# Layer 0 of a two-layer AdaLN block: 32 queries of four heads share a score matmul, and the stage begins in a written order on one load queue

## The chip, the cores and the metric

The kernel runs on one NeuronCore of a Trainium2 chip. The metric is the device time of one execution in microseconds (us). Before the change three runs took 1959.87, 1960.4 and 1962.59 us: a median of 1960.4 us. One core has five engines with queues of their own: TensorE (PE; its weight loads are listed as PEld), VectorE (DVE), ScalarE (ACT), GpSimd (POOL) and SyncE (SP), which here only issues DMAs. SBUF is the working memory of 128 partitions; PSUM has eight banks of 512 f32 columns per partition, into which PE writes.

## The reference, cut to what matters

The program is a two-layer block with adaptive layer norm on 1024 tokens of 512 features, all in f32. The change lies in the first half of layer 0:

```python
mod = (_silu(L0_c) @ L0_wmod).reshape(L0_c.shape[0], 6, 1, -1)
sa, ca, ga, sb, cb, gb = (mod[:, 0], mod[:, 1], mod[:, 2], mod[:, 3], mod[:, 4], mod[:, 5])
...
h = _layernorm(x, axis=-1) * (1 + ca) + sa
x = x + ga * _L0_attn_ref(h, ...)
```

The attention dequantizes its weights (`(qw - 8) * scales`, one scale for 128 rows), makes 32 query heads and 8 key and value heads of 128 features, turns q and k by rotary tables, and computes for each query head

```python
scores = jnp.einsum('bhqd,bhkd->bhqk', q, k) / math.sqrt(HD)
scores = jnp.where(causal[None, None], scores, jnp.finfo(scores.dtype).min)
attn = jax.nn.softmax(scores.astype(jnp.float32), axis=-1).astype(q.dtype)
ctx = jnp.einsum('bhqk,bhkd->bhqd', attn, v)
```

Four query heads (a *group*) share one key and one value head. The context goes through a dequantized output projection. A gated feed-forward network, a second attention with small heads and a mixture of low-rank experts follow; the change does not touch them.

## The kernel before

The code is written for a library that records the operations in program order, works out all dependencies and semaphores, and then lets a planner place the operations on the engines: it takes what is ready by its own model of costs, the earlier in the program the sooner. So each engine's queue is in order on the chip, but that order is the planner's, not simply that of the code. Outside a block of written order (there is none before the change) an operation may be placed ahead of earlier ones. A buffer pool with n buffers makes the n+1st tile wait until the first is released.

**The start** (L92 to L480). `load_x(0)` brings tokens 0 to 511 over SP; x is held as eight tiles of 128 tokens. The vector c arrives twice over ACT's queue, as a column (`cc`, L384) and spread over all partitions (`crow`, L386); then come four tiles `wa` of the modulation weight for the shift (L390) and four tiles `wm` for the scale (`mod_loads`, L117). Each of these tiles is 256 KB. `cc` and `row` are multiplied by their sigmoids. `ln_stats` computes the statistics of four token tiles and the normalized `xn`; `ln_transposes` turns `xn` into four PSUM banks, one of 128 features by 512 tokens each, 16 transposes (L416); the shift comes from 16 matmuls with one moving column each (L446), the scale from four multiply-and-sum operations on DVE (`mod_sums`, L124); `ln_evict` writes hT (L424 on ACT, L429 on DVE). Then follow the first K projection (`project_rope`, L204 on PE; L210, L212, L213 on DVE; the addition L214 on POOL), the V projection (L248), and the same for the second half of the tokens. The loads of weights and tables go over SP (L184, L185, L192, L194, L236, L238).

**The loop over groups.** For each of 8 groups and each of 8 query tiles of 128 (`order`: 7, 0, 6, 1, 5, 2, 4, 3 and, in the last group, 3, 7, 2, 6, 1, 5, 0, 4) a *step* does the following. For each of the four heads `head_probs` streams the (qi+1)*128 keys past that head's 128 queries (L293, pieces of at most 512 columns into a tile of two PSUM banks, three such tiles), adds the causal mask to the last 128 columns (L298), takes the maximum (L300), the exponential with its sum (L303), the reciprocal (L308) and scales (L309). `transpose_probs` transposes blocks of 32x32 in place on DVE (four operations, L315), and 16 DMAs (L317, on SP) carry them into `pT`, with the keys on the partitions. Two steps later `context` (L326) multiplies by v, ACT copies the result (L332), and `project_o` (L337, L342, L343) adds to x. `drain` puts these after the second and the fourth head's scores. The tiles `pr` and `pT` have one buffer for the big steps (qi 4 to 7) and one for the small ones.

**Work beside the steps.** `side_work` prepares the next group: at step 0 the K weight is loaded, at step 1 K is projected, at step 2 V (every second group), at step 3 the first two query heads are projected, at step 5 the third, at step 6 the output weight is loaded and at step 7 the fourth query head is projected. Before the first group all four query heads are projected one after the other (L204), followed by the output weight and the gate. `qT` holds one tile of 1024 columns per head, eight buffers.

In the trace each f32 matmul of the code is two records, the transposes are one.

Of the kernel before, what the change touches and what calls it, by code (L numbers as in the profile page):

```python
# [9 lines left out]
F32 = mybir.dt.float32  # L10
# [3 lines left out]
ALU = mybir.AluOpType  # L14
AX = mybir.AxisListType
# [27 lines left out]
def block_kernel(ctx: ExitStack, tc: tile.TileContext, a: dict, out: bass.AP):  # L43
# [48 lines left out]
    load_x(0)  # L92
# [4 lines left out]
    make_causal_mask(nc, cmask, mask_val=NEG)  # L97
    eps_t = const.tile([P, 1], F32, tag="eps", name="eps_t")
# [66 lines left out]
    with ExitStack() as st:  # L165
# [33 lines left out]
        def project_rope(dst, wf, halves=(0, 1)):  # L199

            for half in halves:
# [11 lines left out]
                nc.vector.tensor_mul(t2[64:128, :], ps[0:64, :], sinT[0:64, sl])  # L213
                nc.gpsimd.tensor_tensor(dst[:, sl], t1, t2, ALU.add)  # L214
# [39 lines left out]
        def project_q(h):  # L254
            qT[h] = qp.tile([P, S], F32, tag="qT", name="qT")
            project_rope(qT[h], wf.pop(("q", h)))
# [12 lines left out]
        class Step:  # L269


            def __init__(self, g, qi):
# [9 lines left out]
                self.pr, self.pT = (  # L282
                    t[:, :used].rearrange("p (b r k i) -> p b r k i", b=NB, r=REP, i=B)
                    for t in (pr, pT)
                )

        def head_probs(u, r):

            nk = u.n * P
            ps = sp.tile([P, S], F32, tag="sc", name="sc")  # L290
            for n0 in range(0, nk, 512):
                w = min(512, nk - n0)
                nc.tensor.matmul(  # L293
                    ps[:, n0 : n0 + w], lhsT=qT[u.g * REP + r][:, bass.ts(u.qi, P)],
                    rhs=kT[u.g][:, n0 : n0 + w], start=True, stop=True,
                )
            dg = ps[:, u.qi * P : nk]
            nc.vector.tensor_tensor(dg, dg, cmask, ALU.add)  # L298
            nb = small.tile([P, 1], F32, tag="nb", name="nb")
            nc.vector.tensor_reduce(nb, ps[:, :nk], AX.X, ALU.max, negate=True)  # L300
            rs = small.tile([P, 1], F32, tag="rs", name="rs")
            pr = u.pr[:, :, r, :, :]
            nc.scalar.activation(  # L303
                pr.rearrange("p b k i -> p k b i"),
                ps[:, :nk].rearrange("p (k b i) -> p k b i", b=NB, i=B),
# [5 lines left out]
        def transpose_probs(u):  # L311

            for b in range(NB):
                t = u.pr[:, b, :, :, :].rearrange("p r k i -> p (r k i)")
                nc.vector.transpose(t, t)  # L315
                for q in range(NB):
                    nc.sync.dma_start(  # L317
                        u.pT[b * B : (b + 1) * B, q, :, :, :].rearrange("p r k i -> p (r k i)"),
                        t[q * B : (q + 1) * B, :],
                    )  # L320

        def context(u):

            ps = psum_mm()
            for kj in range(u.n):
                nc.tensor.matmul(  # L326
                    ps, lhsT=vv[u.g][:, kj, :],
                    rhs=u.pT[:, :, :, kj, :].rearrange("p a r i -> p r a i"),
# [891 lines left out]
```

## Time and profile before

| what | value |
|---|---|
| median of three runs | 1960.4 us |
| the profiled execution | 1962.43 us, of which 1960.7 us from its first to its last instruction (the span) |
| mean granted clock of PE | 0.975 |
| first record on PE | 17.30 us after the start of the span |
| first K projection | 30.44 us |
| first scores | 87.3 us |
| last context of layer 0 | 1143.3 us |
| feed-forward network of layer 0, gate and up | from 1164.2 us |

The page gives busy time per engine, the groups of instructions by code line with their mean length in ns, and the idle time of the engine before them with what ended it. `sc<-kT,qT 128x512` means that the tile sc is written from kT and qT with 512 columns on 128 partitions. The timeline lists start, length, engine, line, operation and count; in brackets is the idle time before, and what ended it. The length of a matmul record includes its way through the array, so two records that follow each other overlap; the distance of their starts is their cost in a row (0.43 us for 512 columns, by 24 records of L204 in 10.46 us).

### The profile page before, as it was taken

Reading aid. Unit: us, or ns where it says so; the run is one execution under the profiler, and the core shown is the slowest. Engines: PE = TensorE matmul, PEld = TensorE weight load, DVE = VectorE, ACT = ScalarE, POOL = GpSimd, SP = SyncE. Lnnn points to the kernel's source line nnn. Section 1 sums busy time; section 2 is a strip of 40 time slices with the busy share of each in tenths; the row PEclk is TensorE's granted clock in tenths of the full one; section 3 lists DMA queues with packets and bytes.
Section 4 is the critical chain, followed back from the end, with each engine's and each line's share of the span. In section 5 each row is a group of like instructions: output and inputs, shape, how many; then the busy total and the mean of one; then the engine's idle time right before and its main releaser. Section 6 shows DMA issues by size and latency. Waiting matters only on the chain.

```text
span 1960.7 us, 21062 instructions
## 1 busy us (share of the span) xinstructions
PE 1842.4 (94%) x6582; PEld 874.5 (45%) x6582; DVE 1175.9 (60%) x2632; ACT 664.5 (34%) x1392; POOL 225.1 (11%) x192
## 2 busy tenths in 40 slices
PE   5989999999999999999998879999988999999987
PEld 4434454444544444544443434444554344334434
DVE  4766757677666767576776542323456577667432
ACT  1134424434334343244335410000113323355530
POOL 0211111111111212111110110002000000000010
PEclk9999999999999999999999989999989889999999
DMA  5344435345533445343444360001001000000001
GB/s 188 118 111 136 122 99 135 91 126 147 132 91 86 112 130 127 99 135 91 127 131 101 87 244 0 0 1 49 0 1 63 8 10 7 4 7 7 5 12 38
DMA packets 93856, 155.77 MB, mean 79 GB/s; under 512 B 25232, under 2 KB 38160, under 8 KB 93744
## 3 DMA queue, kind: packets, MB, share of 16 engines
q1 hardware_dynamic: 91424, 149.17, 28.4%
q10 hardware_dynamic: 1440, 2.36, 0.4%
q0 software_dynamic: 880, 2.88, 0.4%
q8 instruction: 53, 0.87, 0.2%
q14 instruction: 59, 0.48, 0.1%
HBM read 74.38 MB, written 2.36 MB: 39 GB/s over the span
## 4 chain that ended last, share of the span: by engine, by line
PE 71%; DVE 15%; DMA 4%; ACT 4%; issue 3%; SPq 2%; POOL 1%; DVEq 0%; ACTq 0%; POOLq 0%
PE mm L204 10%; PE mm L337 9%; PE mm L326 8%; PE sc L637 8%; PE sc L293 8%; PE sc L821 5%; PE sc L870 4%; PE sc L656 4%; PE ctx L894 3%; PE sc L731 2%; DVE q L832 2%; PE mm L248 2%; DVE nb L300 2%; DVE pr L315 2%; SPq L317 2%
## 5 line engine op out<-in xcount | busy, mean ns | idle before, releaser
L303 ACT ACTIVATE pr<-sc,nb 128x1024 f32<-128x1024 f32 (+7 forms) x256 | 187.6, 735 | 419.5 <-DVE nb L300 319.0
L204 PE MATMUL mm<-hT,wf 128*128 128x512 f32 x640 | 283.4, 594 | 3.1 <-DVE t L213 2.8
L326 PE MATMUL mm<-pT,v 128*128 128x512 f32 x576 | 264.2, 604 | 21.2 <-DMA pT<-pr 21.2
L293 PE MATMUL sc<-kT,qT 128*128 128x512 f32 (+3 forms) x768 | 273.7, 487 | 7.5 <-ACT pr L303 7.5
L337 PE MATMUL mm<-wo,ctxT 128*128 128x512 f32 x512 | 237.7, 603 | 11.4 <-ACT ctxT L332 11.2
L293 PEld LDWEIGHTS sc<-kT,qT 128*128 128x128 f32 x768 | 139.3, 190 | 157.9 <-issue 125.2
L309 ACT ACTIVATE pr<-pr,rs 128x1024 f32<-128x1024 f32 (+7 forms) x256 | 187.9, 768 | 51.7 <-DVE rs L308 51.4
L315 DVE STREAM_TRANSPOSE pr<-pr 128x1024 f32<-128x1024 f32 (+7 forms) x256 | 177.7, 747 | 20.4 <-ACT pr L309 19.3
L300 DVE TENSOR_REDUCE nb<-sc 128x1 f32<-128x1024 f32 (+7 forms) x256 | 187.6, 750 | 3.5
L204 PEld LDWEIGHTS mm<-hT,wf 128*128 128x128 f32 x640 | 121.1, 191 | 153.6 <-issue 142.1
L883 ACT ACTIVATE pspace<-sc 128x512 f32<-128x512 f32 (+3 forms) x303 | 126.9, 503 | 163.6 <-PE sc L877 117.9
L326 PEld LDWEIGHTS mm<-pT,v 128*128 128x128 f32 x576 | 110.0, 194 | 146.9 <-issue 130.5
L832 DVE CUSTOM_DVE_ANT_0 q<-sc,cwide 128x512 f32<-128x512 f32 (+3 forms) x256 | 125.5, 490 | 66.7 <-PE sc L821 42.2
L821 PE MATMUL sc<-kv,q 32*128 32x512 f32 (+3 forms) x768 | 154.5, 536 | 11.2 <-DVE mx L832 9.7
L343 POOL TENSOR_TENSOR x<-x,ot 128x512 f32<-128x512 f32 x64 | 83.1, 1299 | 667.8 <-DVE ot L342 562.9
L637 PE MATMUL sc<-hT,gu 128*128 128x512 f32 x352 | 153.1, 594 | 0.0
L337 PEld LDWEIGHTS mm<-wo,ctxT 128*128 128x128 f32 x512 | 94.6, 191 | 128.4 <-issue 92.6
L870 PE MATMUL sc<-q,kv 32*128 32x512 f32 (+3 forms) x768 | 112.8, 574 | 4.2 <-DVE mx L837 2.0
L214 POOL TENSOR_TENSOR qT<-t,t 128x512 f32<-128x512 f32 x64 | 87.2, 1363 | 175.8 <-DVE t L213 175.8
L308 DVE RECIPROCAL rs<-rs 128x1 f32<-128x1 f32 x256 | 37.6, 156 | 112.7 <-ACT pr L303 111.9
L637 PEld LDWEIGHTS sc<-hT,gu 128*128 128x128 f32 x352 | 66.2, 190 | 85.2 <-issue 79.6
L821 PEld LDWEIGHTS sc<-kv,q 32*128 32x128 f32 x768 | 73.9, 190 | 57.9 <-DVE mx L832 25.9
(174 smaller groups left out, 1763.5 us busy)
## 6 DMA issues: line engine op xcount, KB each, us to landing
pT<-pr SPq DMA_DIRECT2D x128, 128.0 KB, 2.4
pT<-pr SPq DMA_DIRECT2D x128, 112.0 KB, 2.2
pT<-pr SPq DMA_DIRECT2D x128, 96.0 KB, 2.1
wm<-in_wmodT_dram SPq DMA_DIRECT2D x40, 256.0 KB, 2.8
pT<-pr SPq DMA_DIRECT2D x128, 80.0 KB, 2.1
wi<-in_qw_q_dram SPq DMA_DIRECT2D x32, 256.0 KB, 4.1
ws<-in_s_q_dram SPq DMA_DIRECT2D x32, 256.0 KB, 3.8
oi<-in_qw_o_dram SPq DMA_DIRECT2D x32, 256.0 KB, 3.5
```

The source lines that it names most:

```text
L204: nc.tensor.matmul(ps, lhsT=wf[:, c, :], rhs=hT[half][:, c, :], start=(c == 0), stop=(c == NC - 1),)
L293: nc.tensor.matmul(ps[:, n0 : n0 + w], lhsT=qT[u.g * REP + r][:, bass.ts(u.qi, P)], rhs=kT[u.g][:, n0 : n0 + w], start=True, stop=True,)
L300: nc.vector.tensor_reduce(nb, ps[:, :nk], AX.X, ALU.max, negate=True)
L303: nc.scalar.activation(pr.rearrange("p b k i -> p k b i"), ps[:, :nk].rearrange("p (k b i) -> p k b i", b=NB, i=B), AF.Exp, bias=nb, accum ...
L309: nc.scalar.activation(pr, pr, AF.Copy, scale=rs)
L315: nc.vector.transpose(t, t)
L326: nc.tensor.matmul(ps, lhsT=vv[u.g][:, kj, :], rhs=u.pT[:, :, :, kj, :].rearrange("p a r i -> p r a i"), start=(kj == 0), stop=(kj == u.n ...
L337: nc.tensor.matmul(ps, lhsT=u.ctxT[:, r, :], rhs=wo[u.g][:, r, :], start=(r == 0), stop=(r == REP - 1),)
L637: nc.tensor.matmul(ps, lhsT=gu[:, j, m, c, :], rhs=hTc[b][:, c, :], start=(c == 0), stop=(c == NC - 1),)
L821: nc.tensor.matmul(banks[r][:, at : at + w], lhsT=u.q[kp, bass.ts(i, P)], rhs=kT1[kp, u.g, n0 : n0 + w], start=True, stop=True,)
L832: nc.vector.tensor_tensor_reduce(sm[:, :w], ps, cwide[:, 512 - w :], 1.0, -3e38, ALU.add, ALU.max, accum_out=u.mx[:, i, r, 0:1],)
L870: nc.tensor.matmul(banks[r][:, :w], lhsT=kT1[kp, u.g, bass.ts(kb, P)], rhs=u.q[kp, q0:QW], start=True, stop=not diag,)
```

## The change

It has three parts.

1. *The start.* All that is between `ordered = ...manual_schedule()` and `first.close()` keeps, on each engine, the order in which it is written. The loads all go over SP, in the order cc, crow, first half of x, scale weights, shift weights, K weight, tables, V weights, second half of x, second half of the tables, first q weight. The shift is computed as a row: four matmuls with `cc` as the stationary operand and 512 moving columns, a copy to SBUF (`srow`), four transposes of one row each, and a copy to a column. The 16 transposes of `xn` go token tile by token tile. `load_k(0)` is written ahead of the eviction. `ln_stats` is divided in two, and the statistics of the second half lie between two pairs of V projections.

2. *The scores.* `qT` is one tile for a group, with columns ordered by block of 32 queries, then head, then query; POOL writes each head's part in pieces of 32. `probs(u, s)` takes 32 queries of all four heads as the 128 stationary columns, for s = 0 to 3. It streams only the keys up to the last of these queries, (qi*128 + 32s + 32), fills the rest of the last 128 columns with -1e30 on DVE for s < 3, adds a 128x32 mask (`cmask4`, made by four small copies at the start), and takes the maximum over the streamed columns alone. The exponential still covers (qi+1)*128 columns. `pr` and `pT` are laid out anew: the four DVE transposes and the 16 DMAs of a step keep their sizes, and the moving operand of the context matmul is read in pieces of 128 in place of 32.

3. *The fourth query head* is projected at step 5 with the third, and no longer at step 7.

```diff
-    load_x(0)
...
+    cmask4 = const.tile([P, 32], F32, tag="cmask4", name="cmask4")
+    for r in range(REP):
+        rows = slice(32 * r, 32 * r + 32)
+        nc.vector.tensor_copy(cmask4[rows, :], cmask[rows, rows])
...
         def project_q(h):
-            qT[h] = qp.tile([P, S], F32, tag="qT", name="qT")
-            project_rope(qT[h], wf.pop(("q", h)))
+            g, r = divmod(h, REP)
+            if r == 0:
+                qT[g] = qp.tile([P, S // B, REP, B], F32, tag="qT", name="qT")
+            project_rope(qT[g][:, :, r, :], wf.pop(("q", h)))
...
+        def probs(u, s):
+            nk = u.n * P
+            d0 = u.qi * P + B * s
+            ps = sp.tile([P, S], F32, tag="sc", name="sc")
+            q = qT[u.g][:, NB * u.qi + s, :, :].rearrange("p r i -> p (r i)")
+            for n0 in range(0, d0 + B, 512):
+                w = min(512, d0 + B - n0)
+                nc.tensor.matmul(
+                    ps[:, n0 : n0 + w], lhsT=q, rhs=kT[u.g][:, n0 : n0 + w], start=True, stop=True
                 )
...
+            if s + 1 < NB:
+                nc.vector.memset(ps[:, d0 + B : nk], NEG)
+            dg = ps[:, d0 : d0 + B]
+            nc.vector.tensor_tensor(dg, dg, cmask4, ALU.add)
             nb = small.tile([P, 1], F32, tag="nb", name="nb")
-            nc.vector.tensor_reduce(nb, ps[:, :nk], AX.X, ALU.max, negate=True)
+            nc.vector.tensor_reduce(nb, ps[:, : d0 + B], AX.X, ALU.max, negate=True)
...
             elif i == 5:
                 project_q(h0 + 2)
+                project_q(h0 + 3)
             elif i == 6:
                 load_o_weight(g + 1)
-            else:
-                project_q(h0 + 3)
...
+        ordered = first.enter_context(tc.manual_schedule())
         cc = fp.tile([P, NC], F32, tag="cc", name="cc")
-        nc.scalar.dma_start(cc, a["c0"])
+        nc.sync.dma_start(cc, a["c0"])
         row = const.tile([P, D], F32, tag="crow", name="crow")
-        nc.scalar.dma_start(row, a["crow0"].partition_broadcast(P))
+        nc.sync.dma_start(row, a["crow0"].partition_broadcast(P))
+        load_x(0)
+        scales = mod_loads(0, 1, nc.sync)
         wa = []
         for k in range(NC):
             wa.append(fp.tile([P, D], F32, tag=f"wa{k}", name=f"wa{k}"))
-            nc.scalar.dma_start(wa[k], a["wmodS"][bass.ts(k, P), :])
-        scales = mod_loads(0, 1, nc.scalar)
+            nc.sync.dma_start(wa[k], a["wmodS"][bass.ts(k, P), :])
...
-        xn = ln_stats(0)
+        xn = ln_norm(0, *stats)
+        mod_sums(0, 1, scales)
+        ps = psum_mm()
+        for k in range(NC):
+            nc.tensor.matmul(
+                ps[0:1, :], lhsT=cc[:, k : k + 1], rhs=wa[k], start=(k == 0), stop=(k == NC - 1)
+            )
+        srow = fp.tile([1, D], F32, tag="srow", name="srow")
+        nc.scalar.copy(srow, ps[0:1, :])
         banks = ln_transposes(xn)
         ps = psum_mm()
...
+        for c in range(NC):
+            nc.tensor.transpose(ps[:, c : c + 1], srow[:, bass.ts(c, P)], ident[0:1, 0:1])
         mod[0, 0] = const.tile([P, NC], F32, tag="mcol00", name="mcol00")
...
+        nc.vector.tensor_copy(mod[0, 0], ps[:, :NC])
+        load_k(0)
         ln_evict(0, banks)
-        load_k(0)
         load_tables(0)
+        vf, v = load_v(0)
         load_x(1)
-        vf, v = load_v(0)
         load_tables(1)
         kT[0] = kvp.tile([P, S], F32, tag="kT", name="kT")
         project_rope(kT[0], wf["k", 0], (0,))
-        project_v(vf, v, range(4))
-        xn = ln_stats(1)
+        project_v(vf, v, range(2))
+        stats = ln_stats(1)
+        xn = ln_norm(1, *stats)
+        project_v(vf, v, range(2, 4))
```

## The prediction, on record before the change was run

> **What bounds the kernel now.** I read four views in this order: the busy shares and groups of the page, the windows of the layer-0 loop, the waits of TensorE (PE), and the first 45 us as a timeline. The page first:
>
> ```profile
> PE 1842.4 (94%) x6582; PEld 874.5 (45%) x6582; DVE 1175.9 (60%) x2632; ACT 664.5 (34%) x1392; POOL 225.1 (11%) x192
> ...
> L293 PE MATMUL sc<-kT,qT 128*128 128x512 f32 (+3 forms) x768 | 273.7, 487 | 7.5 <-ACT pr L303 7.5
> ```
>
> PE is busy 94% of the span, and the score matmuls (L293) hardly ever wait (7.5 us in 768). A share over the whole span can hide a stage with another limit, so the windows of single groups of the attention come next (columns: length, then busy time of PE, PEld, DVE, ACT, POOL, granted clock, DMA share, GB/s):
>
> ```profile
> 150.00:280.00 130.00, 128.34 (x354) 65.24 (x353) 85.92 (x180) 53.84 (x109) 20.66 (x16) 1.00 0.47 125
> ...
> 410.00:540.00 130.00, 127.90 (x348) 64.18 (x347) 90.37 (x182) 50.95 (x101) 22.34 (x17) 1.00 0.51 135
> ...
> 1040.00:1150.00 110.00, 90.28 (x227) 41.60 (x226) 59.95 (x134) 47.90 (x93) 11.22 (x10) 0.95 0.42 102
> ```
>
> In groups 0 to 6 PE works 128 of 130 us, VectorE (DVE) about 90, ScalarE (ACT) about 53: there PE time taken away is time gained. The last group (from about 1040) has 20 us of PE idle time; the waits say for what:
>
> ```profile
> PE mm L326 <- DMA pT<-pr: 21.2, 5, 7.1
> PE mm L446 <- DMA x<-in_x_dram: 17.3, 1, 17.3
> ```
>
> The context matmuls wait for the transposed probabilities, a latency. The second line is the start of the kernel, the other place where PE does nothing. Its timeline (start, length, engine, line):
>
> ```profile
> 1.64 5.30 ACTq L390 DMA_DIRECT2D wa<-in_wmodS_dram  x4
> ...
> 12.14 1.28 ACT L435 ACT_TABLE_LOAD   x1 [12.14 <-DMA wm<-in_wmodT_dram]
> ...
> 17.30 6.99 PE L446 MATMUL mm<-cc,wa 128*128 128x1 f32 x32 [17.30 <-DMA x<-in_x_dram]
> ...
> 26.44 3.65 PE L416 MATMUL tr<-ident,xn 128*128 128x128 f32 x16 [2.15 <-DVE xn L405]
> ...
> 42.20 1.91 PE L416 MATMUL tr<-ident,xn 128*128 128x128 f32 x16
> ```
>
> ACT issues loads until 12.1 and computes nothing before. DVE, in order, sits behind the second half of x (until 16.49), so cc is multiplied at 17.11 and PE begins at 17.30. The first K projection starts at 30.44.
>
> **Scores (the main term).** Each code matmul is two records in this trace. Shapes of L293, kept apart (busy, mean ns):
>
> ```profile
> L293 PE MATMUL sc<-kT,qT 128*128 128x512 f32 x384 | 187.3, 594 | 4.3 <-ACT pr L303 4.3
> ...
> L293 PE MATMUL sc<-kT,qT 128*128 128x384 f32 x128 | 50.5, 488 | 2.6 <-ACT pr L303 2.6
> ...
> L293 PE MATMUL sc<-kT,qT 128*128 128x128 f32 x128 | 22.5, 274 | 0.0
> ```
>
> 128 columns are worth 594-488 = 106 ns, and (488-274)/2 = 107: 0.835 ns a column. A step now streams (qi+1)*128 columns four times; after the change 128qi+32, +64, +96, +128. That is 96+64+32 = 192 columns less, 160 ns a record, 0.32 us for the two records. But a narrow matmul need not be cheap: L446 took 6.99/32 = 218 ns for one column, L416 3.65/16 = 228 ns for 128 columns, both near each other in the first 30 us, where the same 16 transposes took twice what they took at 42.20 (1.91). One column costs what 128 cost, so the weight load sets a floor at 128 columns. In qi = 0 and qi = 4 all four last pieces are 32 to 128 wide: no gain. Six of eight steps gain, 48 in eight groups: 15.4 us. The six of the last group (1.9) fall where PE waits anyway; I count none of them: **-13.5**. Both ends: without the floor another 16*0.32 = 5.1 (then up to -20.5); with all gain lost to waits, 0.
>
> The Trainium skill ("TensorE: Matmul & The Clock Gate", Back-to-back issue gap) lists about 60 cycles (25 ns) for 1 to 64 columns, so by it the narrow pieces would gain too, about 5 us more. The rows above speak for the floor.
>
> **Beside them on DVE and ACT.** The mask add shrinks from 128x128 (290 ns) to 128x32. A 128x4 add takes 145 to 162, so about 185: 256*105 = 27 us less. The maximum reads 48 columns less on average; from 411 ns (256 wide) to 1222 (1024) it is 1.06 ns a column: 13 us less. New are 192 memsets of 32 to 96 columns in PSUM, an operation that the trace has only in SBUF (85 ns at 32 columns, 59 at one): 112 ns by that slope, at most 290 by the mask row, 21 to 56 us. DVE ends between 19 us less and 16 more, of 90 in 130 us: hidden under PE either way. Exponentials, scaling (row forms with pieces of 32 are already in the 128-wide steps: 396 ns against 360), the transposes and the 16 copies per step keep size and count: 0. q is now written in pieces of 32 on POOL; the trace has no such store. Between today's 1.27 us and twice that, it stays under the 3.43 us that PE needs for a half (8 records of 0.43): 0.
>
> **The start.** The first 8 us move 195 to 408 GB/s, from then on 387 whoever issues, also after 13.4, when SP alone issues. So one queue loses nothing, and the order decides. Adding up 2 us windows: 0.4 MB by 4 us, 0.85 by 6, 1.66 by 8, 2.46 by 10, 3.2 by 12. In the new order x half 0 is complete (1.3 MB) at 7.1, scales (2.4) at 9.7, wa0 (2.6) at 10.4, wa3 (3.4) at 12.4, K weights (3.9) at 13.8. ACT is free to take its tables at once, cc is ready near 4, xn at 10.7 (4 statistics to 8.1, root, 1.9 us of xn). PE then runs 8 records of 512 columns. At the slow start they cost 0.86 each: 10.5 to 17.3 (15.5 if the clock rises on the way); copy of srow 0.6; the 16 transposes beside it 3.4 (or 1.9), 4 small ones 0.8 (0.4); then on DVE the column copy 0.2, which the K dequantization (0.7 to 0.9) is queued behind, and an eviction of 0.8. K starts at 20 to 23.3 instead of 30.44. The chain of half 1 is longer than before (rope 2.1, v eviction, statistics 3.7, xn 1.9, all in order on DVE, PE idle about 2 us before the transposes): K half 1 at 35.7 to 38.7 instead of 43.95, 5 to 8 earlier. I take **-6**, with ends -9 and 0 (the q phase has DVE busy 9.7 to 9.9 of 10 us from 70 on, which may swallow part).
>
> The rule of the same page (Part 1) is that the clock doubles after about 3.4 us of sustained activity; then wa would end at 15.5. Row L446 ran 7 us at 218 ns without rising, which speaks against counting on it; the difference is 1.8 us.
>
> **First scores wait for four heads.** Today heads 0 to 2 are scored at 87.42, while q3's last half leaves POOL at 90.84. DVE gets to the first mask at 89.64 only. New: PE at 90.9, first mask at 92.7, and project_k(1), ready by 85.6, fills PE meanwhile. Context 0 (115.19, after 5.49 idle) comes 1 to 3 us later: **+2** (ends 0 and 5).
>
> **q3 one step sooner.** It issues no load; its 16 records (6.86 us) and six rope multiplies move from step 7 to 5. So steps 7 and the next 0 lose cover. In one group, step 6's last score is at 331.53, its copies land at 347.3 (15.8 us later), and its context begins at 356.47. Of the 24.9 us between, 6.86 go away, 1.6 were idle, 0.3 is saved in scores: 16.1 of work against 15.8. SP needs 22.93 us for the 32 copies of steps 6 and 7 (0.62 to 0.7 each). The margin is gone, hardly more: 0.4 us at 7 boundaries, **+3** (ends 0 and 36).
>
> **Sum**, against the profiled execution (1962.43, span 1960.7 and 1.7 around it): -13.5-6+2+3 = -14.5, 1947.9. The median of the runs is 2.0 below that execution, so the median after should be **1946** (own range 1938 to 1953).
>
> **Rivals.** (1) *Start lost, scores kept*: DVE as the bound at 70 to 90 eats the earlier start. For: 9.85 of 10 us busy. Against: only two slices. -13.5+5 = -8.5: 1952. (2) *Scores not converted*: memset, mask and maximum hold the three score banks longer, and PE waits for the exponential (today 7.5 us) where it had columns. Then -6+5 and a little: 1958. (3) *All better*: no floor, start -9, boundaries free: -13.5-5-9+2: 1935. (4) *Slower*: at each of the 7 boundaries PE runs dry until pT lands. It decides from 2.5 us a boundary (17.5/7). With 3.5 us idle and the half clock that followed such a gap at 601 us (3.4 us at 0.5, 1.7 lost), 7*5.2 = 36: 1978. Against: the chain is 15.8 us under work of 16.1, and the rope multiplies leave it. (5) The written order might not hold on the chip as written, or the planner, which places all that follows, shuffles the loop to a wash: 1960.
>
> **Chances.** Forecast 0.52, (1) 0.17, (2) 0.08, (3) 0.10, (4) 0.08, (5) 0.05. A measurement of this kernel tells 0.2% (4 us) from no change. (2) is half faster, half same: faster 0.83, same 0.08, slower 0.09. The range leaves out (4), (5) and the ends of the others: 1934 to 1958.
>
> **What would show it.** Right: L293 columns 13 to 16 us less busy, idle time before L326 and L293 nearly as now between 150 and 1040; K projection at 20 to 24; first mask near 93. Wrong: L293 busy falls and idle time before L326 at the boundaries grows by more than 2 us each (4); the narrow matmuls well under 110 ns apart (3); DVE at the boundaries without gaps (2).

## The result, and the profile after

The changed kernel takes **1969.1 us** in the median of 19 runs (1964.89 to 1976.76); the kernel before, in the same session, 1961.17 us (19 runs, 1959.3 to 1965.49). The ratio is 1.0041, with a 95% interval of 1.0032 to 1.005. The change makes the kernel 0.4% slower. The forecast was 1946 us, the range ended at 1958: time and sign were wrong. The profiled execution of the changed kernel has a span of 1966.4 us (1960.7 before) and a mean granted clock of 0.969 (0.975).

The page of the changed kernel, in the groups that answer to those shown of before (busy us, mean ns, then the idle time before them and its releaser):

```profile
PE 1836.5 (93%) x6562; PEld 864.1 (44%) x6562; DVE 1165.5 (59%) x2828; ACT 667.0 (34%) x1393; POOL 225.3 (11%) x192
...
L349 PE MATMUL mm<-wo,ctxT 128*128 128x512 f32 x512 | 244.3, 617 | 29.1 <-ACT ctxT L344 28.5
L304 PE MATMUL sc<-kT,qT 128*128 128x512 f32 (+15 forms) x768 | 262.2, 471 | 9.7 <-ACT pr L315 9.0
```

PE is busy 6 us less, the scores 11.5 us less (273.7 to 262.2): most of the forecast saving is there, though the sign that the prediction named was 13 to 16 us. The span is longer all the same, so idle time was added. The waits of PE in the changed kernel (sum, times, longest) say where:

```profile
PE mm L349 <- ACT ctxT L344: 28.5, 26, 2.7
PE mm L338 <- DMA pT<-pr: 20.1, 9, 6.9
PE mm L462 <- DMA wa<-in_wmodS_dram: 11.9, 1, 11.9
```

The wait for pT is what it was (21.2 before), the wait at the start is 5.4 us shorter (the forecast had PE begin at 10.5 us, it began at 11.91). New is the first line: the output projection waits for the copy of the context, 28.5 us. Its counterpart before:

```profile
PE mm L337 <- ACT ctxT L332: 11.2, 17, 2.1
```

The windows of the loop (length, then PE, PEld, DVE, ACT, POOL busy, clock, DMA share, GB/s):

```profile
150.00:280.00 130.00, 125.88 (x344) 63.29 (x343) 83.84 (x202) 54.07 (x109) 18.98 (x15) 0.99 0.46 123
410.00:540.00 130.00, 125.99 (x333) 61.33 (x332) 89.49 (x207) 52.47 (x104) 22.06 (x17) 0.99 0.47 127
1040.00:1150.00 110.00, 90.77 (x230) 41.67 (x228) 63.78 (x176) 51.92 (x102) 10.15 (x8) 0.97 0.40 98
```

PE fell from 128 to 126 of 130 us, and the clock from 1.00 to 0.99. DVE is no busier in the first two, and PE's time in the last group hardly changed. The loss is in groups 0 to 6, and PE does not spend it on work.

**One boundary, side by side.** A *boundary* is the place where step 7 of a group ends and step 0 of the next begins. Here is that of the third group on PE. Before (start, length, engine, line, operation, count; in brackets idle time before and releaser):

```profile
346.17 7.03 PE L204 MATMUL mm<-hT,wf 128*128 128x512 f32 x16
353.04 3.60 PE L293 MATMUL sc<-kT,qT 128*128 128x512 f32 x8
356.47 4.46 PE L326 MATMUL mm<-pT,v 128*128 128x512 f32 x10
360.76 3.60 PE L293 MATMUL sc<-kT,qT 128*128 128x512 f32 x8
364.20 3.60 PE L337 MATMUL mm<-wo,ctxT 128*128 128x512 f32 x8
```

The same window after:

```profile
351.01 4.99 PE L304 MATMUL sc<-kT,qT 128*128 128x512 f32 x12
355.84 4.46 PE L338 MATMUL mm<-pT,v 128*128 128x512 f32 x10
360.13 1.88 PE L304 MATMUL sc<-kT,qT 128*128 128x512 f32 x4
364.69 5.40 PE L349 MATMUL mm<-wo,ctxT 128*128 128x512 f32 x8 [2.69 <-ACT ctxT L344]
```

Before, the fourth query head (16 records) precedes the new step, and the new step's 16 score records stand as 8 ahead of the context and 8 between context and output projection. After, nothing precedes it, and the planner sets 12 ahead and leaves 4 between. The 4 last 1.7 us; then PE is idle for 2.69. ACT in that window, after:

```profile
359.51 2.19 ACT L321 ACTIVATE pr<-pr,rs 128x1024 f32<-128x1024 f32 x2 [0.33 <-DVE rs L320]
361.61 1.09 ACT L315 ACTIVATE pr<-sc,nb 128x1024 f32<-128x1024 f32 x1
...
363.02 1.15 ACT L321 ACTIVATE pr<-pr,rs 128x1024 f32<-128x1024 f32 x1 [0.23 <-DVE rs L320]
364.08 0.57 ACT L344 COPY ctxT<-mm 128x512 f32<-128x512 f32 x1
```

The context is complete at 360.3, but ACT is in order: from 359.5 on it has three scalings and an exponential of the new step ahead of the copy, which begins at 364.08. Before, it began earlier, while PE still had scores to 364.4:

```profile
363.17 0.57 ACT L332 COPY ctxT<-mm 128x512 f32<-128x512 f32 x1
```

After the change, the eight output projections take 5.40 us in place of 3.60, and the clock tells why, in the window of these records:

```profile
364.70:368.30 3.60, 3.60 (x5) 1.58 (x6) 0.16 (x1) 2.20 (x3) 0.00 (x0) 0.54 0.01 3
```

The same gap (2.15, then five of 2.68 or 2.69 us) stands at 220, 365, 494, 636, 764 and 909 us, one for each boundary up to that of group 6; four of the six were followed by 3.4 us at half clock.

**The account of seven groups**, from the first context of group 0 to that of group 7: 936.9 us before, 944.8 after, +7.9. Distances of score records at full clock -13.0 (221.1 to 208.1). Idle time of PE +13.1 (22.4 to 35.5; the wait for ctxT alone 9.4 to 25.6). Lost to half clock +4.2 (8.7 us at half clock, later 17.1). The remaining 3.6 is spread over the other records. The last group takes 91.8 us (91.2), the part behind layer 0 812.5 (812.4), and the first context comes 2.9 earlier.

### The profile page after: what moved, and what is told of

The parts are those of the page before. It is cut to its first block, busy times and chain, and to the rows that moved or that the text cites. A ratio compares the mean times of both kernels' runs of the same rounds, so it can differ in the third digit from the quotient of the medians.

```text
span 1966.4 us, 21175 instructions
## 1 busy us (share of the span) xinstructions
PE 1836.5 (93%) x6562; PEld 864.1 (44%) x6562; DVE 1165.5 (59%) x2828; ACT 667.0 (34%) x1393; POOL 225.3 (11%) x192
## 4 chain that ended last, share of the span: by engine, by line
PE 69%; DVE 16%; ACT 5%; DMA 4%; SPq 3%; issue 2%; POOL 1%; DVEq 0%; POOLq 0%; ACTq 0%
PE mm L208 11%; PE mm L349 9%; PE sc L657 8%; PE mm L338 7%; PE sc L304 6%; PE sc L841 5%; PE sc L890 4%; PE sc L676 4%; PE ctx L914 3%; DVE pr L327 3%; ACT pr L321 2%; DVE nb L312 2%; DVE q L852 2%; SPq L329 2%; PE sc L751 2%
## 5 line engine op out<-in xcount | busy, mean ns | idle before, releaser
L349 PE MATMUL mm<-wo,ctxT 128*128 128x512 f32 x512 | 244.3, 617 | 29.1 <-ACT ctxT L344 28.5
L304 PE MATMUL sc<-kT,qT 128*128 128x512 f32 (+15 forms) x768 | 262.2, 471 | 9.7 <-ACT pr L315 9.0
L312 DVE TENSOR_REDUCE nb<-sc 128x1 f32<-128x384 f32 (+31 forms) x256 | 175.6, 703 | 3.5
L320 DVE RECIPROCAL rs<-rs 128x1 f32<-128x1 f32 x256 | 38.7, 158 | 106.4 <-ACT pr L315 103.8
```

The source lines that it names most:

```text
L304: nc.tensor.matmul(ps[:, n0 : n0 + w], lhsT=q, rhs=kT[u.g][:, n0 : n0 + w], start=True, stop=True)
L312: nc.vector.tensor_reduce(nb, ps[:, : d0 + B], AX.X, ALU.max, negate=True)
L349: nc.tensor.matmul(ps, lhsT=u.ctxT[:, r, :], rhs=wo[u.g][:, r, :], start=(r == 0), stop=(r == REP - 1),)
```

## Experiments

The theory from this profile: **cover**. Without the fourth query head between step 7 and step 0, PE arrives too early and some wait surfaces (work that keeps PE busy while another engine finishes is its cover). Its rivals: the **loop is paced by ACT and DVE**, so saved columns are worth nothing; the **first scores wait for all four heads**; and, as a theory of its own, the **order** of records on PE at the boundary. The letters of the expectations are each text's own. "Seven" is the time from the first context of group 0 to that of group 7, "last" from there to the start of the last context, in the one profiled run of each kernel, in us.

```
variant                                      median us   ratio [95%]              seven  last
before                                       1961.17                              936.9  91.2
after                                        1969.1    1.0041 [1.0032, 1.005]     944.8  91.8
e4  start alone                              1960.98   0.999  [0.9976, 1.0003]    934.2  96.2
e6  scores alone                             1989.78   1.013  [1.0112, 1.0148]    956.3  98.1
e3  fourth head at step 5 alone              1970.26   1.0041 [1.0028, 1.0053]    942.1  94.2
e5  after, old start                         1978.38   1.0077 [1.0062, 1.0092]    941.8  97.8
e1  after, fourth head at step 7             1987.34   1.0125 [1.011, 1.014]      957.3  95.3
e2  after, fourth head at step 6             1958.79   0.9976 [0.9966, 0.9987]    929.1  93.6
e12 after, all columns streamed              1971.71   1.0041 [1.0027, 1.0055]    940.5  94.0
e7  after, context copied by DVE             2019.39   1.0287 [1.0262, 1.0312]    995.8  93.8
e9  after, K projected at step 0             1977.15   1.0083 [1.0057, 1.011]     951.6  91.3
e10 after, hold                              1971.93   1.0041 [1.0026, 1.0056]    933.5 101.7
e11 e2 and hold                              1962.01   0.9994 [0.9984, 1.0005]    928.8 102.9
e14 after, hold in groups 0 to 6             1955.86   0.9958 [0.9942, 0.9974]    933.1  92.7
e13 after, fourth head in halves, 6 and 7    1957.0    0.9977 [0.9967, 0.9988]    929.7  93.8
e15 e13 and hold in groups 0 to 6            1947.44   0.9918 [0.9902, 0.9934]    923.2  96.2
e16 before, start, fourth head at step 6     1963.41   0.9998 [0.9989, 1.0007]    937.5  92.8
e17 before, hold in groups 0 to 6            1975.29   1.0062 [1.0047, 1.0077]    946.4  94.0
e18 before, start, halves, hold              1972.98   1.0052 [1.0036, 1.0067]    948.1  95.3
```

Two things for reading the table. Many expectations missed: the times of e1, e3, e5, e6, e7, e9, e14, e17 and e18 lie outside every range that they gave, those of e2 and e15 by less than 1 us. And the part behind layer 0, the same code in all variants, took from 808.9 us (e15) to 816.8 (e10) in the profiled runs, 812.4 before and 812.5 after, with 74 to 98 us at half clock. So differences of a few us between medians need not come from the edit; where it matters, the column "seven" decides.

### The three parts alone

**e4**, the kernel before with part 1 of the diff alone.

> The kernel before with the first part alone: written order and one load queue. In the changed kernel the query projections began 6.6 us earlier (48.4 for 55.0). Theory A and B alike: the loop is as before, so 1961 - 6.6 = 1954 to 1955; if DVE at 60 to 90 us eats it, 1957 to 1961.

1960.98 us; the interval of the ratio includes 1. The first context comes 6.8 us earlier (108.4), the seven groups gain 2.7, but the last group takes 5.0 more and the part behind layer 0 3.9 more (816.3 against 812.4, with 98 against 81 us at half clock). What the start gains arrives at the loop, and most of it is not in the end; why the later stages took longer in that run is not settled.

**e6**, part 2 alone (old start, fourth head at step 7).

> The kernel before with the second part alone: 32 queries of four heads in a score matmul, the fourth query head at step 7, old start. The streamed columns fall by 19 to 20 us by the distances of the records in the changed kernel. Theory A: nearly all of that is gained, less 2 to 5 us because the first scores wait for four heads: 1944 to 1949. Theory B: the wait for ctxT appears here, 1962 to 1975. A third theory, C: with four heads in a piece the projection at step 7 itself stands in the way of the next group's first scores (rope and POOL before them, about 4 us a group): 1961 - 20 + 28 = 1965 to 1972, with the idle time before L293's successor and not before the output projection.

1989.78, the slowest of the parts. The waits of PE:

```profile
PE sc L305 <- POOL qT L222: 20.9, 8, 3.2
PE mm L350 <- ACT ctxT L345: 18.8, 27, 2.1
```

Six of the eight waits are of 3.24 us, at the boundaries up to that of group 6: the first stacked scores need the fourth head, whose last half POOL stores only then (from 359.19 to 360.95 us, for scores that begin at 361.01). The rival of the four heads holds wherever the fourth head stands at step 7.

**e3**, part 3 alone.

```diff
                 project_q(h0 + 2)
+                project_q(h0 + 3)
             elif i == 6:
                 load_o_weight(g + 1)
-            else:
-                project_q(h0 + 3)
```

> The kernel before with the third part alone: the fourth query head is projected at step 5, scores per head as before, old start. Theory A: the boundary wait appears here too, so PE's wait for ctxT rises from 11 to about 30 us and the time by 15 to 30 us: 1976 to 1991. Theory B: no new wait, 1957 to 1965.

1970.26, 0.41% slower, with the scores and the start of before.

```profile
PE mm L337 <- ACT ctxT L332: 20.2, 26, 1.7
```

The wait for ctxT goes from 11.2 to 20.2 us, that for pT does not move (20.4). At the boundaries the planner writes the same order as in the changed kernel, 12 score records ahead of the context and 4 behind it, with gaps of 1.63 to 1.75 us. The fourth head's step alone costs 8 us, of which, by the profiled runs, 5.2 lie in the seven groups and 3.0 in the last. Moving it is what makes part 2 usable, and it has a price of its own.

**e5** and **e1**, the changed kernel without part 1, and without part 3 (the fourth head back at step 7).

> The changed kernel with the old start (parts two and three alone). The kernel with the start alone was 2 us faster than the one before, inside its interval, though its first context came 6.8 us earlier; the changed kernel's came 2.9 earlier. If the start is worth what the trace shows at the first context, this kernel is 3 to 6 us slower than the changed one: 1972 to 1975; if half-clock stretches later give it back, 1967 to 1971.

> The changed kernel with its third part undone: the fourth query head is projected at step 7 again. Theory A (the moved projection): the 6.9 us of PE work that stood at step 7 were the time in which ACT and DVE caught up before the next group's first step; without them the copy of the context to ctxT sits behind the exponentials on ACT and PE waits (2.69+0.68+0.30+0.56 = 4.2 us a group, and often a half clock of 3.4 us after the longest). Then this kernel loses that wait at seven boundaries: 1969 - 7*(3 to 4) = 1941 to 1948. Theory B (the stacked scores themselves cause the wait: three banks are held by pieces that all end at nearly the same time, and memset, mask and maximum come between): this kernel keeps the wait of ctxT near 28 us and lies within 4 us of 1969.

1978.38: in the changed kernel the new start is worth 0.36%, 7 us. 1987.34: the same eight waits for POOL's qT (20.9 us) as in e6.

**e2**, the fourth head at step 6, between the two.

```diff
             elif i == 5:
                 project_q(h0 + 2)
-                project_q(h0 + 3)
             elif i == 6:
+                project_q(h0 + 3)
                 load_o_weight(g + 1)
```

> The changed kernel with the fourth query head projected at step 6, between the places tried so far (5 in the changed kernel: PE waits 2.7 us for ctxT at a group boundary; 7 in the run before: PE waits 3.2 us for q from POOL). Theory A+C (the projection is the only spare PE work near the boundary: too late it stands before the first scores, too early it leaves the copy of the context behind the exponentials): at step 6 its rope and POOL work end 9 us before the next scores, and step 7 begins 6.9 us later, so step 0 meets an ACT that has caught up. No wait for POOL, and the wait for ctxT falls from 28 to 15 us or less: 1950 to 1958. Theory B (the stacked scores stall at the boundary wherever the projection is): 1964 to 1975.

1958.79, 0.24% faster than before. Up to the boundary of group 6 none has a gap of over 0.7 us; the seven groups take 929.1, 15.7 less than in the changed kernel, for the same instructions. The boundary of the third group on PE:

```profile
350.27 2.47 PE L304 MATMUL sc<-kT,qT 128*128 128x416 f32 x6
352.57 4.46 PE L338 MATMUL mm<-pT,v 128*128 128x512 f32 x10
356.87 3.54 PE L304 MATMUL sc<-kT,qT 128*128 128x512 f32 x8
360.25 3.60 PE L349 MATMUL mm<-wo,ctxT 128*128 128x512 f32 x8
```

Moving this one line turns the sign. But two things change with it: the projection stands nearer to the boundary, and the planner sets 8 score records between context and output projection again. Of the variants without the hold introduced below, those with the fourth head at step 5 (after, e3, e5, e7, e9, e12) all have 12 and 4, the others all 8 in between.

### What paces the boundary

**e12**, all (qi+1)*128 columns streamed and the maximum taken over them, with four 128x128 masks and no memset: the stacked scores without their saving.

```diff
-            for n0 in range(0, d0 + B, 512):
-                w = min(512, d0 + B - n0)
+            for n0 in range(0, nk, 512):
+                w = min(512, nk - n0)
...
-            if s + 1 < NB:
-                nc.vector.memset(ps[:, d0 + B : nk], NEG)
-            dg = ps[:, d0 : d0 + B]
-            nc.vector.tensor_tensor(dg, dg, cmask4, ALU.add)
+            dg = ps[:, u.qi * P : nk]
+            nc.vector.tensor_tensor(dg, dg, cmask4[s], ALU.add)
```

> The changed kernel without the saving of columns: pieces of 32 queries of four heads, but all (qi+1)*128 keys streamed, one mask of 128x128 for each of the four pieces, no memset, the maximum over all columns. PE has 17 us more to stream. If PE sets the pace in the loop, 1969 + 17 = 1983 to 1987. If the loop waits on the chain over ACT and DVE at the boundaries, PE's longer scores fill the gaps: 1966 to 1975, with less idle time before the output projection.

The same ratio, 1.0041. In the changed kernel the whole saving is worth nothing: with 13.6 us more of score records in the seven groups (208.1 to 221.7), these take 4.3 us less (940.5), the boundary gaps shrink from 2.69 us to between 1.63 and 1.75, and no half clock follows them. PE is not what sets the pace at that place.

**e7**, the copy of the context on DVE, to take it out of ACT's queue.

```diff
-            nc.scalar.copy(u.ctxT.rearrange("p r q -> p (r q)"), ps)
+            nc.vector.tensor_copy(u.ctxT.rearrange("p r q -> p (r q)"), ps)
```

> The changed kernel with the copy of the context to ctxT on DVE in place of ACT (DVE about 0.4 us for 256 columns from PSUM, so 0.7 for 512). Theory A: what PE waits for at the boundary is a place in ACT's queue, behind the exponentials of the next group's first step. On DVE the copy stands behind shorter work (maxima of 1.2 us), so the wait for ctxT falls, by 7*2 us and the half clocks that follow: 1950 to 1960. If not the place in the queue counts but the whole load of ACT and DVE at the boundary, the wait moves to DVE and the time stays at 1965 to 1973.

2019.39, 2.9% slower.

```profile
PE sc L304 <- ACT pr L315: 48.5, 23, 4.4
PE mm L349 <- DVE ctxT L344: 29.5, 17, 3.4
```

On DVE, in order too, the copy stands behind reciprocals that wait for ACT's exponentials (3.28 us idle ahead of one at 375.9 us) or behind 4.6 us of transposes, and the masks and maxima behind it come later, so the scores wait for their banks. It is again a short copy in a queue of longer work.

**e9**, the K weight loaded a group ahead and K projected at step 0 in place of 1.

> The changed kernel with other PE work at the boundary: the K weight is loaded one group ahead at step 6, and K is projected at step 0 in place of step 1 (same 16 records, 6.9 us, not needed before the next group). In this kernel's order they stand right behind the first output projection of the group. Theory A: spare work at the boundary is what is missing. The first wait for ctxT (2.69) stands before these records on PE and may stay, the following ones (0.68, 0.3, 0.56) go: 1960 to 1967. If PE's order takes them before the output projection, 1948 to 1955.

1977.15, worse. The gaps for ctxT remain (23.6 us, longest 2.7): the 16 records of K stand behind the copy that is waited for. Work helps only if it stands ahead of it.

### The order on PE

**e10** and **e11**: the third score matmul of each step (s = 2) may be issued only behind the last context matmul before it. So at most 8 of the 16 large score records go ahead of a context, and 8 stay behind it. e10 is the changed kernel with this hold, e11 is e2 with it.

```diff
+                with tc.issue_after(held[0].ins) if s == 2 and held[0] is not None else ExitStack():
                     nc.tensor.matmul(
                         ps[:, n0 : n0 + w], lhsT=q, rhs=kT[u.g][:, n0 : n0 + w],
                         start=True, stop=True,
                     )
...
-                nc.tensor.matmul(
+                held[0] = nc.tensor.matmul(
                     ps, lhsT=vv[u.g][:, kj, :],
```

> The changed kernel with one order fixed by hand: the third score piece of a step is queued on PE behind the last context matmul of that step. In the changed kernel the planner puts three of the four pieces of a group's first step ahead of the context, so only four records (1.7 us) are left between the context and the output projection, which waits 2.7 us for the copy to ctxT; in the kernel before it was eight (3.4 us). Theory A1 (the wait is this order): the wait at the boundary falls under 1.3 us at once and the time to 1955 to 1961. Theory A2 (as my prediction priced its rival: without the projection at step 7 the transposed probabilities are not there in time): PE now waits in front of the context for pT by about as much, and the time stays at 1965 to 1973.

> The kernel with the projection at step 6 (1958.8, wait for ctxT 18 us) with the same order fixed by hand. There the planner had put the third piece behind the context already at the boundary, so A1 expects little: 1953 to 1960. If holding pieces back costs elsewhere (ACT gets its exponentials later in every step), 1961 to 1968.

1971.93 and 1962.01: nothing gained. The first reading, that the order does not matter, was wrong, and only the division by groups shows it. (In e11 the seven groups stay where e2 has them, 928.8 and 929.1: there 8 records already stood between.) In e10 the seven groups gain 11.3 us (944.8 to 933.5) and the last group loses 9.9 (91.8 to 101.7): there PE waits for pT anyway, and the hold keeps the scores from filling that wait. The waits of e10:

```profile
PE mm L342 <- DMA pT<-pr: 34.5, 12, 8.2
...
PE mm L353 <- ACT ctxT L348: 11.1, 14, 1.7
```

**e14** takes the hold out of the last group alone (`if s == 2 and u.g + 1 < NKV and ...`).

> The changed kernel; in groups 0 to 6 the third score matmul of a step (s of 2) is issued only behind the last context matmul before it, as in the run with the hold in all groups; group 7 keeps the planner's order. In that run the seven groups took 933.5 us from first context to first context (944.8 in the changed kernel), and the last group 101.7 (91.8). Theory D (the loss in groups 0 to 6 is an order in which too few scores stand between context and output projection; the hold's own cost fell in the last group alone): the seven groups near 934, the last near 92, so 1959 to 1963 us. Theory A (cover is lost, and the hold only exchanges one wait for another): seven groups at 940 to 945, 1966 to 1972 us.

1955.86, 0.42% faster than before and 0.8% faster than the changed kernel. The seven groups as in e10, 11.7 us under the changed kernel, the last at 92.7: the order is a cause by itself. Its boundary on PE:

```profile
354.54 3.33 PE L305 MATMUL sc<-kT,qT 128*128 128x512 f32 x8
359.19 4.53 PE L342 MATMUL mm<-pT,v 128*128 128x512 f32 x10 [1.31 <-DMA pT<-pr]
363.55 3.54 PE L305 MATMUL sc<-kT,qT 128*128 128x512 f32 x8
366.93 3.60 PE L353 MATMUL mm<-wo,ctxT 128*128 128x512 f32 x8
```

8 and 8 again: no gap at ctxT, and in its place one of 0.8 to 1.8 us at pT, the wait that the prediction had named. Behind the order the missing cover appears. By two single runs it is the smaller part: e2, with 8 between as well and no wait for pT at these boundaries, is another 4.0 us lower in the seven groups (933.1, 929.1).

**e13** gives it back without the wait of e1: the half of the tokens that the next group's first step reads is projected at step 6, the other at step 7.

```diff
             elif i == 6:
+                project_q(h0 + 3, (0,) if g + 2 == NKV else (1,))
                 load_o_weight(g + 1)
+            elif i == 7:
+                project_q(h0 + 3, (1,) if g + 2 == NKV else (0,))
```

> The changed kernel, but the fourth query head is projected in two halves: the half of the tokens that the next group's first step reads at step 6, the other half at step 7 (8 records each, so cover stands ahead of the boundary again, and the first scores of the next group wait only for the half of step 6). Theory A (the boundary has lost its cover, and some wait surfaces there, of the copy of ctxT or of pT): the gap of 2.7 us before L349 at the boundary shrinks to under 1 us, no wait for POOL's qT of over 1 us appears, 1950 to 1957 us, at least 0.4% under the kernel before and not above the variant with the whole head at step 6 (1958.8). Theory B (what is lost is lost in the loop as a whole, on ACT and DVE, wherever the fourth head stands): 1958 to 1968 us, with the waits moved elsewhere. Theory C (the first scores wait for the whole of POOL's qT whatever half they read): 1980 to 1990 us with seven waits of about 3 us for POOL's qT.

1957.0, no better than e2 within the intervals; no wait for POOL over 0.7 us, so the scores do wait only for the half that they read. The 0.4% that the first theory asked for was not reached. Waits of 0.3 to 2 us for ctxT remain, 18.6 us in all.

**e15**, e13 and e14 together.

> The variant with the fourth query head in two halves (steps 6 and 7; 1957.0 us, seven groups 929.7), with the same hold in groups 0 to 6. Theory A (with cover in place the order no longer matters): seven groups at 928 to 931, 1955 to 1959 us. Theory D (the order costs wherever the fourth head stands): the smaller waits for ctxT go too, seven groups at 920 to 926, 1948 to 1954 us.

**1947.44 us**, ratio 0.9918 (0.9902 to 0.9934), the seven groups 923.2. It beats both kernels. Its boundary on PE:

```profile
348.10 3.60 PE L208 MATMUL mm<-hT,wf 128*128 128x512 f32 x8
351.53 1.77 PE L305 MATMUL sc<-kT,qT 128*128 128x512 f32 x4
353.14 4.46 PE L342 MATMUL mm<-pT,v 128*128 128x512 f32 x10
357.43 3.54 PE L305 MATMUL sc<-kT,qT 128*128 128x512 f32 x8
360.81 3.60 PE L353 MATMUL mm<-wo,ctxT 128*128 128x512 f32 x8
```

No bracket: with 8 records of cover ahead and 8 scores between, neither wait ends last. Idle time in the seven groups is 20.4 us (22.4 before, 35.5 in the changed kernel), with the columns saved. Of the 14.5 us between the profiled runs of before and e15, 13.7 lie in the seven groups and 2.2 ahead of them; the last group takes 5.0 more, and 3.5 fall behind layer 0, where nothing was edited. Why the hold gains 6.5 us in the seven groups on e13 and nothing on e2 is not shown.

### What the stacked scores are worth

**e16** is e4 with the fourth head at step 6; **e17** the kernel before with the hold in groups 0 to 6; **e18** is e15 with the old scores of one head each.

> The kernel before with the new start and the fourth query head at step 6, but with the old scores of one head each. It stands beside the variant of the change with the fourth head at step 6 (1958.8 us, seven groups 929.1): the difference is what the stacked scores are worth where the boundary has its cover. Theory E (the 11 to 13 us of streaming that are saved in groups 0 to 6 reach the end): 1962 to 1968 us, seven groups at 936 to 941. Theory B (they are swallowed by waits): 1956 to 1961 us, seven groups at 928 to 933.

> The kernel before with the hold alone (groups 0 to 6: the third head's score matmul is issued only behind the last context matmul before it). Theory D (the hold mends an order that the stacked scores and the early fourth head brought about; in the kernel before eight score records stand there already): within 0.3% of the kernel before, 1958 to 1969 us. Theory F (the hold is worth its 11 us by itself, whatever the scores): 1950 to 1955 us.

> The variant at 1947.4 us (new start, fourth head in two halves at steps 6 and 7, hold in groups 0 to 6) with the old scores of one head each: the difference to that variant is what the stacked scores are worth once order and cover are right. Theory E (the streaming saved reaches the end in full, 11 to 13 us in groups 0 to 6): 1958 to 1963 us, seven groups at 934 to 937 (923.2 there). Theory B (part of it is still swallowed by waits): 1950 to 1956 us, seven groups at 926 to 932.

e16: 1963.41, seven groups 937.5 where e2, with stacked scores, has 929.1. The saved columns are worth something where 8 records stand between: 8.4 of some 13 us.

e17 and e18 came out above every bound given: 1975.29 and 1972.98. With the old scores the hold costs 9 to 11 us in the seven groups (946.4 against 936.9; 948.1 against 937.5 of e16, which has the whole head at step 6), so the gain of e15 is not the hold's by itself. It also means that the 24.9 us between e18 and e15 is no measure of the scores: hold and stacked scores act together. The traces show where the time went: in e17 PE is idle 4.9 us more than before in the seven groups and at half clock for 18.0 us (8.7 before), in e18 1.8 more than in e16 and 21.1 (5.7). Why the hold does this to the old scores was not followed up. The fairest figure for stacked scores, fourth head and hold together is e15 against e4, which has the start alone: 934.2 to 923.2 in the seven groups, 0.72% of the time between the two ratios.

## Why the prediction was wrong, point by point

- **"there PE time taken away is time gained"**: true of the share, not of the place. e12 shows that the saved columns were worth nothing in this order, e16 with e2 that they are worth 8.4 us in another. PE's 98% in the window hid that at the boundary the next release is ACT's.
- **Scores, -13.5**: the term itself was right; the distances of score records fell by 13.0 us in the seven groups. The floor came out right as a sum: the fastest step with qi = 0 went from 0.884 to 0.861 us of score records, that with qi = 4 from 4.321 to 4.268, where 0.32 would have gone without a floor. It is no floor of each record, though. Behind a wide record, the first of the two records of a 32, 64 or 96 column matmul costs 28, 56 and 83 ns by the distance of the starts; the second costs 112, as at 128 columns. Where narrow matmuls follow each other (qi = 0), the first costs 139. The Trainium skill ("TensorE: Matmul & The Clock Gate", Back-to-back issue gap) lists one figure, about 25 ns, for 1 to 64 columns; here the 28 ns come near it, the 56 and the 112 do not.
- **DVE, between 19 less and 16 more**: mask 68.7 to 45.3, maximum 187.6 to 175.6, memsets 19.8; 15.6 less in sum. The memset in PSUM took 85, 112 and 138 ns for 32, 64 and 96 columns, the mask 193 (forecast 185). Inside its ends, with the memsets just under their 21 to 56.
- **The start, -6**: right at its own place. The timeline of the changed kernel on PE:

```profile
11.91 6.02 PE L462 MATMUL mm<-wa,cc 128*1 128x512 f32 x8 [11.91 <-DMA wa<-in_wmodS_dram]
17.86 1.97 PE L431 MATMUL tr<-ident,xn 128*128 128x128 f32 x16
...
21.84 2.38 PE L208 MATMUL mm<-hT,wf 128*128 128x512 f32 x5 [1.69 <-DVE hT L444]
```

  K begins at 21.84 (forecast 20 to 23.3), its second half at 37.23 (35.7 to 38.7), the query projections are 6.65 us earlier. **First scores wait for four heads, +2**: of the 6.65 the first context keeps 2.9, where the start alone keeps 6.8 (e4). So the other parts cost some 3.9 there, inside the term's ends. The first mask came at 85.79 us, not near 93: the sign as written had left out that the start was earlier. In the end the start is worth 7 us in the changed kernel (e5) and not a measurable amount alone (e4).
- **"q3 one step sooner ... The margin is gone, hardly more: 0.4 us at 7 boundaries, +3"**: this is the step that failed. It compared one chain, the 15.8 us from the last score to pT, with the work beside it, and the wait for pT indeed stayed as it was. But a second chain ends at the same place: context, copy on ACT, output projection. The fourth head stood ahead of both. With it gone ahead to step 5 the planner filled the space with the new step's own scores, so that 4 records in place of 8 were left to cover the copy, and their exponentials and scalings stood ahead of the copy on ACT. The part alone measured +8 (e3). In the changed kernel 13.1 us of idle time, 4.2 of half clock and 3.6 spread over other records, 20.9 in sum, stand against what the scores saved in the seven groups, where 3 was forecast. One step later for the fourth head takes back 15.7 of it (e2), the order alone 11.7 (e14).
- **Rival (4)** had the place (the boundaries), the sign and the half clock behind a gap, at 0.08; the gaps of 2.69 us lie near the 2.5 a boundary that it needed to turn the sign, under the 3.5 of its price. It named the wrong releaser, pT. The sign by which it was to be known, idle time before L326, did not appear; it stood before the output projection. Part of rival (2) holds as well: in this order the scores were not converted (e12), but through the copy, not through the score banks, whose waits hardly moved (7.5 to 9.0 us).
- **Costing an order as fixed.** The prediction took the order of records around the boundary as that of before, with 16 removed. The planner wrote another one. Rival (5), at 0.05, had said that the planner might shuffle the loop, to a wash; it gave no place and no cost.

What stays open: why the planner's order came out as 12 and 4; why the hold hurts the old scores (e17, e18); and why the last group and the later stages took 5.0 and 3.9 us more in the profiled run of e4, more at half clock than before.

## What to carry to other kernels

When work is moved away from a place where the engine that bounds the kernel is full, list every chain that ends there, not only the longest: each had the same cover, and the one that surfaces may be another engine's queue in which a short copy stands behind new long work. A planner fills the hole with what is ready, so look at how many instructions are left between a producer and its consumer; an edit that forces that number, or that leaves half of the moved work behind, may be worth more than the saving itself. Read a change that acts in a loop by groups: e10's total hid +11 and -10.

## What the runs showed of the hardware that was not expected

**Half clock after short gaps.** In the loop between 130 and 1030 us, a stretch of 3.4 or 6.8 us at half clock began within a gap of PE or up to 2 us behind it in 28 of 39 cases for gaps over 2.5 us, in 14 of 26 for 1.9 to 2.5, in 10 of 83 for 1.2 to 1.9 and in none of 53 for 0.7 to 1.2, counted over the profiled runs of all the kernels here. A stretch of 3.4 us loses about 1.7 us by this clock. The Trainium skill ("TensorE: Matmul & The Clock Gate", HAM oscillation) warns of idle gaps above some 3.4 us; here shorter ones sufficed, not each time. The runs of the changed kernel, which are spread over 12 us where those of before are spread over 6, go with it: the three longest (1974.67 to 1976.76 us) had a mean granted clock of 0.965 to 0.967, the three shortest (1964.89 to 1965.23) of 0.969 to 0.972. That they go together does not show which causes which.

**The ramp at the start.** Eight records of 512 columns from 11.91 us on took 6.02 us, 0.75 each, between the 0.43 of full clock and 0.86, twice that; the 16 transposes behind them took 1.97 us, as long as at full clock (1.91). Before the change 32 one-column records had taken 6.99 us, and the same 16 transposes after them 3.65.
